# Batching and ending of a grouped convolution behind a chain of 18 pointwise layers

## The chip, the cores and the metric

The kernel runs on one core of one Trainium2 chip. The metric is the device time of one execution in microseconds (us). The engines are TensorE (PE, with its weight loads as PEld), VectorE (DVE), ScalarE (ACT), GpSimd (POOL) and SyncE (SP, which issues DMAs). All data is fp32.

## What is computed

The input `x` is 32 images of 14 x 14 pixels with 512 channels. Two layers follow each other, and each adds to its input:

```python
def layer0(x):                       # after a group norm of x, 32 groups
    anchors = []
    for i in range(18):
        nx = gelu(x @ block_w[i] + block_b[i])          # 512 x 512
        if i in (11, 14, 17):
            h = gelu(mean(nx) @ fc1_w[t] + fc1_b[t])
            gates = softmax((h @ fc2_w[t] + fc2_b[t]).reshape(-1, 3, 512), axis=1)
            nx = nx + gammas[t] * sum_a(gates[a] * anchors[a])
        x = nx
        if i in (1, 4, 9): anchors.append(x)
    return x
x = x + layer0(_gn(x))
x = x + conv3x3(_gn(x), W, groups=32)                   # SAME padding
```

`_gn` normalizes every image over each group of 16 channels.

## The kernel before, in words

**Blocks.** Channels lie on the 128 partitions, in four chunks `c` of 128; pixels lie on the free axis. A "tile" n is two images (392 pixels), a pair p is two tiles, so there are 8 pairs of 4 images. A block is one of the 18 layers for one pair; there are 144, and `steps` (lines 90 to 99) fixes their order: neighbouring pairs are interleaved so that the gating of one pair runs under blocks of the other. The last six blocks are 15 to 17 of pair 6 and then 15 to 17 of pair 7. A block multiplies 2 x 2 half matrices with 7 products in place of 8 (`block`, line 352): each product is 4 matmuls of 128 x 128 by 392 columns, and each fp32 matmul shows as two rows in the trace. ACT saves intermediate sums and applies the gelu, DVE adds PSUM into them (L403) and forms four differences of the inputs of the next block (L350). A `quarter` is a buffer of two chunks by 392 pixels; 35 of them serve everything that lives for a while.

**The calendar.** All other work is put by hand between the products. A block has seven ticks, one after each product, so the n-th block begins at tick 7n; `tend` is the tick after the last. `at(tick, fn)` books a function, and `put(first, {"dve": us, "act": us}, fn)` books it at the first tick from `first` on where the room of each engine named (`ROOM` per tick of a block, `TAIL` from `tend` on) still holds its estimate. At build time the ticks are run in order, so the calendar sets the order of the instructions on each engine's queue and on SP's, and each engine works its queue in order.

**Gating** (`plan_gates`, line 563). After a target layer (11, 14, 17), `gate_hidden` and `gate_logits` compute the gates from the pooled output; `gate_part` adds two of the three gated anchors on DVE, one image and one chunk at a time (L542), and `gate_last` scales the third on ACT (L554), added by `gate_add` (L561).

**End of a pair** (`plan_end`, line 651). After layer 17 the pair's input, kept in HBM (`xkeep`), is loaded and added (`load_residual`, `residual`, L605 and L609). DVE takes the statistics (`bn_stats` and `bn_aggr`, L183 and L184). Means and variances are averaged over groups by a matmul with a mask (`scales_mean`, `scales_rstd`), the power -0.5 is taken on POOL (L205), and a Newton step follows (`scales_newton`). ACT writes two sets of columns, `x` itself (L619) and the normalized one (L624), into an order that has the image column outermost, and two DMAs for each chunk and set (L636) write them to HBM, to `x2d` and `xnd`, once for the left and once for the right eight columns of the image. For the last pair these DMAs are issued by ACT, else by SP.

**Convolution.** A group of 16 input and 16 output channels with 8 image columns fills 128 rows; the filter row and the image column become a band matrix of 128 x 128 for each of the three filter rows. These bands are built once (`build_band`) and kept in HBM (`band`). A batch is half of the images (`NBAT` 2, 16 images), and a unit is one group of a batch, so there are 64 units. A unit loads its normalized columns, its `x` and its bands (L738, L745; for batch 1 the bands are loaded ahead by `load_bands`, L726), does six matmuls (L756, three filter rows for the left and right halves), adds `x` (L766), transposes (L780), and copies into an output tile on ACT (L787). After eight units, a chunk, ACT issues the output's DMAs (L794).

**Order of the units** (`plan_batch`, line 817, and lines 885 to 892). Batch 0, ready when pair 3 is done, has 32 units; 14 are spread over the blocks, and `NLATE` 18 run from `tend` on. Batch 1 is ready when pair 7 is done:

```python
        else:
            for j in range(NG // 2):
                at(a + 1 + j // 2, load_bands, j)
            for g in range(NG):
                plan_unit(m, g, b + 3 + g, 4)
```

Here `b` is one tick after the last columns of the last pair, so all 32 units follow it. Loads are booked three to eight ticks ahead, but not before their ring of buffers comes free: in `plan_unit` four for bands, five for normalized columns, six for `x`.

Of the kernel before, what the change touches and what calls it, by code (L numbers as in the profile page):

```python
# [19 lines left out]
def kernel(  # L20
# [84 lines left out]
    ROOM = {"dve": (1.5, 0.0, 3.3, 3.3, 1.2, 0.0, 0.0), "act": (1.0, 0.4, 1.5, 1.5, 0.8, 0.4, 0.0)}  # L105
    TAIL = {"dve": 4.0, "act": 3.6}
# [67 lines left out]

    def stats_tiles(name):
        st = small.tile([P, NR, 6], F32, tag="st", name=f"st_{name}")
        mv = small.tile([P, NR, 2], F32, tag="mv", name=f"mv_{name}")
        return {"st": st, "mv": mv}

    def stats_of(d, xc, c, n, images=range(NI)):  # L180
        for b in images:
            r = c * NB4 + n * NI + b
            nc.vector.bn_stats(d["st"][:, r, :], xc[:, b * HW : (b + 1) * HW])  # L183
            nc.vector.bn_aggr(d["mv"][:, r, :], d["st"][:, r, :])  # L184

    def scales_mean(d, name):
        mv = d["mv"]
        mps = aux(f"mps_{name}")
        nc.tensor.matmul(mps[:, :NR], lhsT=gmask, rhs=mv[:, :, 0], start=True, stop=True)
        mr = small.tile([P, 3, NR], F32, tag="mr", name=f"mr_{name}")  # L190
        nc.vector.tensor_copy(mr[:, 0], mps[:, :NR])
        v3 = small.tile([P, NR], F32, tag="v3", name=f"v3_{name}")
        nc.vector.tensor_sub(v3, mv[:, :, 0], mr[:, 0])
        nc.vector.tensor_mul(v3, v3, v3)
        nc.vector.tensor_add(v3, v3, mv[:, :, 1])
        d["mr"], d["v3"] = mr, v3

    def scales_rstd(d, name):

        vps = aux(f"vps_{name}")  # L200
        nc.tensor.matmul(vps[:, :NR], lhsT=gmask, rhs=d["v3"], start=True, stop=True)
        ve = small.tile([P, NR], F32, tag="ve", name=f"ve_{name}")
        nc.vector.tensor_scalar(ve, vps[:, :NR], 1e-5, None, ALU.add)
        y = small.tile([P, NR], F32, tag="y", name=f"y_{name}")
        nc.gpsimd.tensor_tensor(y, ve, mhalf, ALU.pow)  # L205
        d["ve"], d["y"] = ve, y

    def scales_newton(d, name):
        ve, y = d["ve"], d["y"]
        e = small.tile([P, NR], F32, tag="e", name=f"e_{name}")  # L210
        nc.vector.tensor_mul(e, y, y)
        nc.vector.tensor_mul(e, e, ve)
        nc.vector.tensor_scalar(e, e, -0.5, 1.5, ALU.mult, ALU.add)
        mr = d["mr"]
        nc.vector.tensor_mul(mr[:, 1], y, e)
        if name[0] == "b":
            nc.vector.scalar_tensor_tensor(
                mr[:, 2], mr[:, 0], -1.0, mr[:, 1], ALU.mult, ALU.mult
            )
# [56 lines left out]
    def plan_start(p):  # L276
# [16 lines left out]
        b = put(b + 1, {"dve": 0.8}, lambda: scales_mean(pst[p], f"a{p}"))  # L293
        b = put(b + 1, {"dve": 0.2}, lambda: scales_rstd(pst[p], f"a{p}"))
        b = put(b + 2, {"dve": 0.8}, lambda: scales_newton(pst[p], f"a{p}"))
# [147 lines left out]

    fcw = {}
# [46 lines left out]
    def gate_logits(k, t, name, box):  # L491
# [3 lines left out]
        for m in range(NCK, NL):  # L495
# [30 lines left out]
        gt = small.tile([P, NA, NC4], F32, tag="g", name=f"g_{name}")  # L526
        nc.vector.scalar_tensor_tensor(
            gt, ex, gam[:, t : t + 1], sm.unsqueeze(1).to_broadcast([P, NA, NC4]),
            ALU.mult, ALU.mult,
# [3 lines left out]
    def gate_part(p, box, h, n, d):  # L533

        gt = box["g"]
        c = h * NH + d
        for b in range(NI):
            sl = slice(b * HW, (b + 1) * HW)
            j = c * NB4 + n * NI + b
            o = box["nx"][h][n][:, d, sl]  # L540
            for a in range(NA - 1):
                nc.vector.scalar_tensor_tensor(  # L542
                    o, anc[p][a][h][n][:, d, sl], gt[:, a, j : j + 1], o, ALU.mult, ALU.add
                )

    def gate_last(p, i, box, h, n):

        gt = box["g"]
        q = box[h, n] = quarter(f"gq{h}{n}_{p}_{i}")
        for d in range(NH):  # L550
            for b in range(NI):
                sl = slice(b * HW, (b + 1) * HW)
                j = (h * NH + d) * NB4 + n * NI + b
                nc.scalar.activation(  # L554
                    q[:, d, sl], anc[p][NA - 1][h][n][:, d, sl], AF.Identity,
                    scale=gt[:, NA - 1, j : j + 1],
                )

    def gate_add(box, h, n):
        nx = box["nx"]  # L560
        nc.vector.tensor_tensor(nx[h][n], nx[h][n], box.pop((h, n)), ALU.add)  # L561

    def plan_gates(p, i):

        k = at_step[p, i]
        t1 = NP7 * (k + 1)
        name = f"{p}_{i}"
        ti = TARGETS.index(i)
        box = boxes[p, i] = {}
        end = k == len(steps) - 1  # L570
        if p == 0:
            at(t1 + 1, gate_differences, k, ti)
        at(t1 + (0 if end else 1), gate_hidden, k, ti, name, box)
        a = put(t1 + (1 if end else 2), {"dve": 2.6}, gate_logits, k, ti, name, box) + 1
        last = a
        for n in range(2):
            for h in range(2):
                b = put(a, {"act": 1.4}, gate_last, p, i, box, h, n)
                for d in range(NH):
                    last = max(last, put(a, {"dve": 1.65}, gate_part, p, box, h, n, d))  # L580
                last = max(last, put(b + 1, {"dve": 0.95}, gate_add, box, h, n))
        assert i == NB - 1 or last < NP7 * at_step[p, i + 1], (p, i, last)
        return last
# [3 lines left out]
    NBAT = 2  # L587
# [6 lines left out]
    x2d, xnd = [  # L594
        [
            [tc.dram_tile([2, P * KC, NV], F32, name=f"{v}{m}_{c}") for c in range(NCK)]
            for m in range(NBAT)
        ]
        for v in ("x2d", "xnd")
    ]  # L600

    def load_residual(p, n, h, d):
        t = 2 * p + n
        d[n, h] = quarter(f"xb_{t}_{h}")
        nc.sync.dma_start(d[n, h].rearrange("p c n -> p (c n)"), xkeep[t][h])  # L605

    def residual(n, h, p, d):
        nx = boxes[p, NB - 1]["nx"]
        nc.vector.tensor_add(nx[h][n], nx[h][n], d.pop((n, h)))  # L609

    def columns(p, c, n, d, mr=None):
# [3 lines left out]
        if n == 0:  # L615
            d[c] = qpool.tile([P, W, PV], F32, tag="q", name=f"xc{mr is None:d}_{p}_{c}")
        src = nx[c // NH][n][:, c % NH, :].rearrange("p (q w) -> p w q", w=W)
        if mr is None:
            nc.scalar.copy(d[c][:, :, n * NI * H : (n + 1) * NI * H], src)  # L619
        else:  # L620
            for b in range(NI):
# [3 lines left out]
                    d[c][:, :, q0 : q0 + H], src[:, :, b * H : (b + 1) * H], AF.Identity,  # L625
                    scale=mr[:, 1, r : r + 1], bias=mr[:, 2, r : r + 1],
                )
        if n == 0:
            return
        xc = d.pop(c)  # L630
        m, j = divmod(p, BP)
        dest = (x2d if mr is None else xnd)[m][c]
        for v in range(2):
            w0 = v * (W - KC)
            eng = nc.scalar if p == NPAIR - 1 else nc.sync
            eng.dma_start(  # L636
                dest[v].rearrange("(q k) v -> q k v", k=KC)[:, :, j * PV : (j + 1) * PV],
# [3 lines left out]
    def plan_residual(p, a):  # L641

        xb = {}
        last = a
        for h in range(2):
            for n in range(2):
                at(a - 2, load_residual, p, n, h, xb)
                last = max(last, put(a, {"dve": 1.0}, residual, n, h, p, xb))
        return last

    def plan_end(p, a):
        d, xc, xd = {}, {}, {}

        def stats(n, c):
            if not d:
                d.update(stats_tiles(f"b{p}"))
            stats_of(d, boxes[p, NB - 1]["nx"][c // NH][n][:, c % NH], c, n)

        at(a, anc.pop, p)
        if p < NPAIR - 1:  # L660
            a = plan_residual(p, a)
        last = a
        for c in range(NCK):
            for n in range(2):
                last = max(last, put(a, {"dve": 1.0}, stats, n, c))
        b = put(last + 1, {"dve": 0.8}, lambda: scales_mean(d, f"b{p}"))
        b = put(b + 1, {"dve": 0.2}, lambda: scales_rstd(d, f"b{p}"))
        b = put(b + 2, {"dve": 0.8}, lambda: scales_newton(d, f"b{p}"))
        b += 1
        for c in range(NCK):  # L670
            for n in range(2):
                put(a, {"act": 0.95}, columns, p, c, n, xc)
        for c in range(NCK):
            for n in range(2):
                b = put(b, {"act": 0.95}, lambda c=c, n=n: columns(p, c, n, xd, d["mr"]))
        return b
# [6 lines left out]
    band = [tc.dram_tile([P, 3 * P], F32, name=f"band{g}") for g in range(C // CG)]  # L683
# [12 lines left out]
    def build_band(g):  # L696
# [4 lines left out]
        tiles = [  # L701
            cvpool.tile(shape, F32, tag="xn", name=f"bt{v}_{g}", bufs=NXN) for v in range(2)
        ]
# [225 lines left out]
```

## Time and profile before

| what | value |
|---|---|
| median of 3 runs | 3023.99 us (3022.62 to 3025.87) |
| the profiled execution | 3026.72 us, span 3025.0 us |
| PE, PEld busy | 2940.5 us (97%), 1802.0 us (60%) |
| DVE, ACT, POOL busy | 1810.6 us (60%), 1520.8 us (50%), 47.9 us (2%) |
| mean granted TensorE clock | 0.990 |
| moved by DMA | 456.74 MB, mean 151 GB/s |

The span runs from the first to the last instruction of the core. The page shows it in 40 equal slices of about 76 us; a digit is the busy share of a slice in tenths, and `PEclk` is the clock that TensorE was granted. A row of busy times by stage gives, for a stretch of the span, the busy microseconds of each engine with the number of its instructions, then the clock (1.00 is full), the mean busy share of the 16 DMA engines, and GB/s. A row of the timeline gives start, duration, engine and line, operation, output and inputs, how many instructions it merges, and in brackets the idle time before it and what ended it. A row of groups gives busy time and mean duration in ns, and after the second bar the idle time before the group.

### The profile page before, as it was taken

How to read it: one execution, taken by the hardware profiler on the slowest of the kernel's cores; microseconds unless marked ns; L12 is line 12 of the kernel's file. 1: busy time of each engine (PE TensorE's matmuls, PEld its weight loads, DVE VectorE, ACT ScalarE, POOL GpSimd, SP SyncE). 2: the span in 40 equal slices, each digit the busy share in tenths (PEclk: the TensorE clock that was granted, in tenths of full speed). 3: DMA queues.
4: the chain of work that ended last, by engine and by line, in shares of the span. 5: the costliest groups of instructions: out<-in, count | busy, mean ns of one | idle time of the engine just before them, and what ended most of it. 6: DMA issues, size and time to landing. Idle time of an engine off the chain costs nothing.

```text
span 3025.0 us, 32202 instructions
## 1 busy us (share of the span) xinstructions
PE 2940.5 (97%) x9985; PEld 1802.0 (60%) x9985; DVE 1810.6 (60%) x3679; ACT 1520.8 (50%) x3603; POOL 47.9 (2%) x25
## 2 busy tenths in 40 slices
PE   7999999999999999999999999999999999999758
PEld 4555555555565555555565566666566655665657
DVE  5466565776567766776667564774557633666711
ACT  3444445556455555556455554555555554555442
POOL 0000000000000000000000000000000000000000
PEclk9999999999999999999999999999999999999979
DMA  4343334545454544645454444544446444334895
GB/s 141 120 146 132 126 118 156 182 126 151 151 160 140 164 128 142 190 129 155 134 165 144 146 129 138 190 125 142 134 140 191 139 141 131 124 127 137 256 284 165
DMA packets 404595, 456.74 MB, mean 151 GB/s; under 512 B 151899, under 2 KB 239050, under 8 KB 404426
## 3 DMA queue, kind: packets, MB, share of 16 engines
q1 hardware_dynamic: 361994, 437.38, 46.3%
q10 hardware_dynamic: 42432, 17.32, 2.3%
q8 instruction: 80, 1.31, 0.2%
q14 instruction: 89, 0.73, 0.1%
HBM read 372.83 MB, written 81.79 MB: 150 GB/s over the span
## 4 chain that ended last, share of the span: by engine, by line


## 5 line engine op out<-in xcount | busy, mean ns | idle before, releaser
L366 PE MATMUL x<-t,s 128*128 128x392 f32 x2304 | 808.1, 493 | 0.0
L379 ACT ACTIVATE o<-c,bias 128x392 f32<-128x392 f32 x720 | 440.2, 620 | 568.2 <-DVE c L403 551.7
L366 PEld LDWEIGHTS x<-t,s 128*128 128x128 f32 x2304 | 434.0, 190 | 306.1
L399 ACT COPY c<-x 128x392 f32<-128x392 f32 x576 | 279.5, 485 | 393.7 <-PE x L366 386.2
L366 PE MATMUL z<-t,s 128*128 128x392 f32 x1152 | 404.7, 494 | 0.0
L366 PE MATMUL x<-t,w 128*128 128x392 f32 x1152 | 402.7, 492 | 0.0
L366 PE MATMUL z<-o,s 128*128 128x392 f32 x1088 | 381.7, 494 | 0.0
L366 PE MATMUL y<-o,w 128*128 128x392 f32 x1088 | 381.4, 493 | 0.0
L366 PE MATMUL x<-o,w 128*128 128x392 f32 x1088 | 380.3, 492 | 0.0
L403 DVE TENSOR_TENSOR c<-x,c 128x392 f32<-128x392 f32 x288 | 160.0, 564 | 347.7 <-PE x L366 290.9
L403 DVE TENSOR_TENSOR c<-y,c 128x392 f32<-128x392 f32 x288 | 163.3, 567 | 330.5 <-PE y L366 223.2
L366 PEld LDWEIGHTS x<-t,w 128*128 128x128 f32 x1152 | 218.9, 190 | 160.3
L542 DVE SCALAR_TENSOR_TENSOR o<-o,g,o 128x196 f32<-128x196 f32 x768 | 298.7, 420 | 14.2
L366 PEld LDWEIGHTS z<-t,s 128*128 128x128 f32 x1152 | 216.0, 190 | 148.9
L350 DVE TENSOR_TENSOR t<-o,o 128x784 f32<-128x784 f32 x272 | 264.1, 971 | 67.4 <-ACT o L379 64.8
L366 PEld LDWEIGHTS x<-o,w 128*128 128x128 f32 x1088 | 206.6, 190 | 149.7
L366 PEld LDWEIGHTS z<-o,s 128*128 128x128 f32 x1088 | 204.7, 190 | 144.2
L366 PEld LDWEIGHTS y<-o,w 128*128 128x128 f32 x1088 | 204.6, 190 | 143.9
L350 DVE TENSOR_TENSOR t<-o,t 128x784 f32<-128x784 f32 x272 | 264.4, 972 | 5.5
L403 DVE TENSOR_TENSOR c<-z,c 128x392 f32<-128x392 f32 x288 | 158.8, 562 | 106.5 <-PE z L366 105.7
L399 ACT COPY c<-z 128x392 f32<-128x392 f32 x288 | 138.9, 482 | 162.8 <-PE z L366 162.4
L379 ACT ACTIVATE o<-x,bias 128x392 f32<-128x392 f32 x240 | 140.3, 585 | 91.6 <-PE x L366 85.0
(102 smaller groups left out, 1966.1 us busy)
## 6 DMA issues: line engine op xcount, KB each, us to landing
w<-in_L_conv_block_w_dram SPq DMA_DIRECT2D x144, 1024.0 KB
s<-skeep SPq DMA_DIRECT2D x504, 256.0 KB
skeep<-s SPq DMA_DIRECT2D x72, 256.0 KB
xn<-xnd SPq DMA_DIRECT2D x64, 224.0 KB
xs<-x2d SPq DMA_DIRECT2D x64, 224.0 KB
xkeep<-xt SPq DMA_DIRECT2D x32, 392.0 KB
xb<-xkeep SPq DMA_DIRECT2D x32, 392.0 KB
x2d<-xc SPq DMA_DIRECT2D x56, 224.0 KB
```

The source lines that it names most:

```text
L350: nc.vector.tensor_tensor(t[j], i0, i1, ALU.subtract)
L366: nc.tensor.matmul(acc[d][:, :N], lhsT=lhsT[:, kk, d * P : (d + 1) * P], rhs=rhs[:, kk, :], start=first and kk == 0, stop=kk == NH - 1, sk ...
L379: nc.scalar.activation(o[:, d, :], srcs[d], AF.Gelu_apprx_tanh, bias=bias[:, r : r + 1])
L399: nc.scalar.copy(cs[d], acc[d][:, :N])
L403: nc.vector.tensor_tensor(cs[d], acc[d][:, :N], cs[d], ALU.add)
L542: nc.vector.scalar_tensor_tensor(o, anc[p][a][h][n][:, d, sl], gt[:, a, j : j + 1], o, ALU.mult, ALU.add)
```

## The change

Six things change together.

1. **Four batches of 8 images, two groups a unit.** `x2d` and `xnd` become one array in which `x` and the normalized columns (index e) and the left and right half (v) lie side by side for each row, so that a unit needs one load. Each batch has 16 units of two groups; bands are kept for two groups together. Two band buffers and five buffers for columns serve all batches but the last, whose bands are loaded ahead.
2. **The last pair ends chunk by chunk**: gates, statistics, scales and columns of chunk 0, then of chunk 1, and so on; units of the last batch wait for their chunk only. All writes of columns are issued by SP.
3. **Gates on differences.** Since the gates sum to one, `gates @ anchors` is anchor 0 plus two gated differences. Anchors 1 and 2 are turned into differences in place, once for each pair; `gate_base` adds gamma times anchor 0 before the gates are known.
4. **x is added by a DMA** that accumulates into the output of the last layer, issued by POOL after `gate_base`.
5. **Statistics without `bn_aggr`**: the two halves that `bn_stats` gives go into the group sums, with two matmuls each.
6. **Room and late units**: `ROOM` and `TAIL` change, and 14 units of batch 2 run from `tend` on.

The diff, cut to its core:

```diff
-    ROOM = {"dve": (1.5, 0.0, 3.3, 3.3, 1.2, 0.0, 0.0), "act": (1.0, 0.4, 1.5, 1.5, 0.8, 0.4, 0.0)}
-    TAIL = {"dve": 4.0, "act": 3.6}
+    ROOM = {"dve": (1.7, 0.0, 3.4, 3.4, 1.7, 0.0, 0.0), "act": (1.0, 0.8, 1.5, 1.5, 1.0, 0.8, 0.8)}
+    TAIL = {"dve": 3.0, "act": 3.6}
...
-            nc.vector.bn_aggr(d["mv"][:, r, :], d["st"][:, r, :])
...
+    def group_sums(name, src, n):
+        ps = aux(name)
+        for v in range(2):
+            nc.tensor.matmul(
+                ps[:, :n], lhsT=gmask, rhs=src[:, :, v], start=v == 0, stop=v == 1
+            )
+        return ps[:, :n]
...
+    def anchor_difference(p, a, h, n):
+        v = anc[p][a][h][n]
+        nc.vector.tensor_tensor(v, v, anc[p][0][h][n], ALU.subtract)
+
+    def gate_base(p, i, h, n):
+
+        t = TARGETS.index(i)
+        o = boxes[p, i]["nx"][h][n]
+        nc.vector.scalar_tensor_tensor(
+            o, anc[p][0][h][n], gam[:, t : t + 1], o, ALU.mult, ALU.add
+        )
+
+    def gate_part(p, box, c, n, b):
+
+        h, d = divmod(c, NH)
+        sl = slice(b * HW, (b + 1) * HW)
+        j = c * NB4 + n * NI + b
+        o = box["nx"][h][n][:, d, sl]
+        nc.vector.scalar_tensor_tensor(
+            o, anc[p][1][h][n][:, d, sl], box["g"][:, 0, j : j + 1], o, ALU.mult, ALU.add
+        )
...
+        box["base"] = {
+            (h, n): put(t1, {"dve": 1.0}, gate_base, p, i, h, n) for h in range(2) for n in range(2)
+        }
+        return put(t1 + (1 if end else 2), {"dve": 2.2}, gate_logits, k, ti, name, box) + 1
+
+    def plan_gates(p, t, a, chunks):
+
+        box = boxes[p, t]
+        last = max(a, *box["base"].values())
+        for cs in chunks:
+            for n in range(2):
+                b = a
+                for c in cs:
+                    b = put(b, {"act": 0.75}, gate_last, p, t, box, cs, c, n)
+                for c in cs:
+                    for i in range(NI):
+                        last = max(last, put(a, {"dve": 0.43}, gate_part, p, box, c, n, i))
+                last = max(last, put(b + 1, {"dve": 0.5 * len(cs)}, gate_add, box, cs, n))
         return last
...
-    NBAT = 2
+    NBAT = 4
...
+    def residual(n, h, p):
+
+        nc.gpsimd.dma_start(
+            boxes[p, NB - 1]["nx"][h][n].rearrange("p c n -> p (c n)"),
+            xkeep[2 * p + n][h], accum_op=ALU.add,
+        )
...
+    def plan_end(p):
+
+
+        d = {}
+        for (h, n), tick in boxes[p, NB - 1]["base"].items():
+            at(tick, residual, n, h, p)
         if p < NPAIR - 1:
-            a = plan_residual(p, a)
-        last = a
+            a = gated[p] + 1
+            at(a, anc.pop, p)
+            return [plan_norm(p, d, a, list(range(NCK)))] * NCK
+        a = gated[p]
+        out = []
         for c in range(NCK):
...
+            b = plan_gates(p, NB - 1, a, [[c]])
+            if c == NCK - 1:
+                at(b + 1, anc.pop, p)
+            out.append(plan_norm(p, d, b, [c]))
+        return out
...
-    NXS, NXN, NBW = 6, 5, 4
...
+    NX, NBW = 5, 2
...
+    def unit_load(m, u):
+
+        c, ul = divmod(u, UC)
+        xs = cvpool.tile([P, 2, 2, 2 * NV], F32, tag="x", name=f"x_{m}_{u}", bufs=NX)
+        nc.sync.dma_start(
+            xs.rearrange("r g e n -> r g (e n)"),
+            x2d[m][c].rearrange("(g r) e v n -> r g (e v n)", r=P)[:, 2 * ul : 2 * ul + 2],
+        )
+        if m == NBAT - 1:
+            bw = bands.pop(u)
+        else:
+            bw = cvpool.tile([P, 2, 3, P], F32, tag="bw", name=f"bw_{m}_{u}", bufs=NBW)
             nc.sync.dma_start(
...
+                bw.rearrange("p g y d -> p (g y d)"), band[u].rearrange("p g n -> p (g n)")
+            )
+        units[m, u] = {"xs": xs, "bw": bw}
...
+        ready = ended[(m + 1) * BP - 1]
+        if m < NBAT - 1:
+            t0 = ready[-1] + 6
+            t1 = ended[(m + 2) * BP - 1][-1] if m < NBAT - 2 else tend - 4
+            early = NU - (NLATE if m == NBAT - 2 else 0)
+            for u in range(early):
+                plan_unit(m, u, t0 + (t1 - t0) * u // early, 8)
+            for j in range(NU - early):
+                left["dve"][tend + 1 + j] += 0.65
+                left["act"][tend + 2 + j] += 0.9
+                plan_unit(m, early + j, tend + j, 3)
         else:
-            for j in range(NG // 2):
-                at(a + 1 + j // 2, load_bands, j)
-            for g in range(NG):
-                plan_unit(m, g, b + 3 + g, 4)
+            tk = 0
+            for u in range(NU):
+                tk = max(tk + 1, ready[u // UC] + 3, tend + NLATE)
+                at(tend + (u - 6 if u < 6 else 3 + u // 2), load_bands, u)
+                plan_unit(m, u, tk, 3)
...
-    NLATE = 18
+    NLATE = 14
```

Here `plan_norm` books the statistics, scales and columns of the chunks that it is given, NU is 16 units of a batch, UC is 4 units of a chunk, and `ended` holds for each pair the tick of the last columns of each chunk.

## The prediction

> **What bounds the kernel now.** I read the page's slices first, then the busy time by stage, then the timeline of the end, then the groups by shape.
>
> ```profile
> PE   7999999999999999999999999999999999999758
> PEclk9999999999999999999999999999999999999979
> DMA  4343334545454544645454444544446444334895
> ```
>
> PE is full until about slice 37; only then do the DMA engines fill up and does PE fall back. So there are two stages with different bounds. By stage:
>
> ```profile
> core 0: us, PE busy (x) PEld busy (x) DVE busy (x) ACT busy (x) POOL busy (x), PEclk, DMA share, GB/s
> 75.00:2812.00 2737.00, 2736.55 (x8993) 1628.93 (x8993) 1700.58 (x3396) 1423.06 (x3287) 37.70 (x13) 1.00 0.46 145
> 2812.00:2835.00 23.00, 19.50 (x118) 17.99 (x119) 19.38 (x47) 9.62 (x38) 0.00 (x0) 1.00 0.70 205
> 2835.00:2920.00 85.00, 40.89 (x198) 35.78 (x196) 30.87 (x108) 38.69 (x96) 5.80 (x2) 0.75 1.00 258
> 2920.00:2985.00 65.00, 60.04 (x329) 57.99 (x330) 12.43 (x20) 16.14 (x80) 0.00 (x0) 0.90 0.95 285
> 2985.00:3025.00 40.00, 29.82 (x185) 28.89 (x183) 7.45 (x12) 9.30 (x52) 0.00 (x0) 0.91 0.31 83
> ```
>
> From 75 to 2812 us (the blocks) PE idles 0.45 us in 2737: DVE (62% busy) and ACT (52%) never end a wait that matters, so relief of them there is worth nothing, and **every PE instruction moved into this stage costs its full time**. The end is 213 us, from the last product at 2812 to 3025: until 2920 the DMA engines are full and PE is half idle, then PE runs 32 units in a row.
>
> ```profile
> 2861.99 2.65 SPq L745 DMA_DIRECT2D bw<-band  x1
> ...
> 2870.73 4.36 PE L756 MATMUL cps<-xn,bw 128*128 128x224 f32 x12 [3.57 <-DMA bw<-band]
> ...
> 2920.21 7.39 PE L756 MATMUL cps<-xn,bq 128*128 128x224 f32 x24 [21.34 <-DMA xn<-xnd]
> 2923.63 1.25 ACTq L636 DMA_DIRECT2D xnd<-xc  x2
> 2927.87 2.33 PE L756 MATMUL cps<-xn,bq 128*128 128x224 f32 x12
> ...
> 3011.43 2.33 PE L756 MATMUL cps<-xn,bq 128*128 128x224 f32 x12
> ...
> 3016.29 1.08 ACTq L794 DMA_DIRECT2D out_dram<-o  x1
> ```
>
> A load of bands issued at 2862 lets PE go on at 2870.7; PE then waits 21 us for normalized columns, because all of batch 1 (32 units) sits behind the last pair's columns (last write issued 2924). Units then come every 2.60 us (3008.83 to 3011.43, say), and from the last unit's matmuls to the end it is 13.6 us (2.6 of matmuls, 11.0 after).
>
> **The change, part by part.**
>
> *Units.* Before, 14 units of 64 run inside the blocks and 50 after. A unit after the change (two groups of 8 images) has the same 6 matmuls and 4 transposes as one before (one group of 16), so 64 again. Following the planner's arithmetic, batches 0 and 1 fit inside the blocks (32 units); batch 2 is ready early too, but only 2 of its 16 are placed there, 14 are kept for the end (NLATE). So 34 inside, 30 after: 20 units move into the full PE stage, **20 x 2.60 = +52 us**.
>
> *Group sums.* Mean and variance become two matmuls each: 2 more per set, some 15 sets inside the blocks. Such a matmul is two PE rows, 0.36 us at most (L189 in the timeline), 0.22 from start to start. 30 x 0.22 to 0.36 = 7 to 11 us; I take 7. The last product then ends at 2812 + 52 + 7 = 2871.
>
> *Vector and Scalar work.*
>
> ```profile
> L542 DVE SCALAR_TENSOR_TENSOR o<-o,g,o 128x196 f32<-128x196 f32 x768 | 298.7, 420 | 14.2
> L624 ACT ACTIVATE xc<-o,mr_b 128x196 f32<-128x196 f32 x128 | 85.1, 725 | 9.1 <-issue 9.1
> L619 ACT COPY xc<-o 128x392 f32<-128x392 f32 x64 | 55.0, 876 | 8.6 <-issue 8.6
> L184 DVE BATCH_NORM_AGGREGATE mv_a<-st_a 128x2 f32<-128x6 f32 x128 | 23.3, 182 | 4.4
> ```
>
> DVE loses 384 gate parts (161 us), 256 aggregates (47) and 32 additions of x (31); it gains 64 differences of anchors at 0.97 (62) and 96 base steps, which no row shows at this size: 0.97 (the 128x784 addition) to 4 x 0.42, so 93 to 161. Net 16 to 84 us less, all beside PE: 0. The planner allows DVE 10.2 us a block instead of 9.3; with its own 7.3 us (4 x 0.97 + 6 x 0.565) that is 17.5 of the block's 18.5, so the cover is thin, and I put 0 to 10 us of stalls into the range.
>
> *The accumulating DMA.* It replaces a plain load and an addition. The new wait: the first gate part stands at the head of DVE's queue until it has landed, with the additions of PSUM (L403), and so PE's banks, behind. Between base step and first gate part lie 4 ticks of 2.64 us = 10.5 us. No DMA from POOL is in the trace. Its packets are those of the load of x (3136 B, median 124 ns, 8 on each engine: 1.0 us, perhaps double for an accumulate). Here a rule speaks against the change: the Trainium skill (SBUF — State Buffer, "SBUF: two separate sides") says that one-source fp32 copies of VectorE in two-port mode lock GpSimd out of writing descriptors; the section after it tells of a POOL DMA of 620 ns that became 3100. At 4 us undisturbed (my estimate: the row, twice over, plus issue and landing as the 3.4 us of a band below) a fivefold 20 us would miss the slack by 10, for 7 pairs: 70 us. But the rows around it are DVE instructions with two inputs or a PSUM source (L350, L403, L542), which that page doesn't count as two-port ("Who interferes with whom"). I take 0, with 70 as the far bound; it is nearer 0. On POOL's queue the powers of the scales (2.90 us, L205) come behind it, due 14 ticks later and more: 0.
>
> *The end.* Per DMA, from the packet records of the trace (medians: 224 B 16 ns, about 18 in the mixed stretches; 512 B 27; 896 B 42; 1536 B 65; 2048 B 84; 3136 B 124) on 16 engines. The new unit load has 256 packets of 1792 B (75 ns between those rows): 1.20 us; two groups' bands 128 x 3072 B (121 ns): 0.97; a write of columns 1024 x 224 B: 1.15; an output 1568 x 512 B: 2.65. In the order of SP's queue, from the last product to the load of unit 7 of batch 3, which stands behind the last pair's last columns: 12 units of batch 2 (26.0), 8 loads of batch 3 (9.6), 10 bands (9.7), 32 writes of pairs 6 and 7 (36.8), 4 outputs (10.6), 4 accumulations (4.0): **96.7 us**. The same count over 2835 to 2920, dips included, gives 0.90 of the time, and 1.0 in pure reads (2930 to 2950); I take 0.94: 103 us. Plus 1.5 to start and 2 to land: 106.5. The last pair's writes leave ACT's queue (8 of x, 8 of the normalized; an issue held ACT 0.5 to 2.4 us) for SP's, which then waits for the columns with later unit loads behind; those are issued three ticks ahead, so 0 while the DMA queues are full.
>
> Nine units (7 to 15) are then left: 23.4 us, since their loads (1.2 each, an output per four) come faster than PE's 2.60. The first two run slow, as at 2920: 24 rows in 7.39 us instead of 4.6, +2.8. The skill (TensorE: Matmul & The Clock Gate, Part 1) releases the clock after about 3.4 us of work, which would make it some 1.7; the trace decides, 2.8. Before, PE lost another 8 us to output buffers in 32 units (2920.2 to 3013.8 less 83.2 and 2.8): +2 here. Last step 11.0. The end is 106.5 + 23.4 + 2.8 + 2 + 11.0 = **146 us** instead of 213.
>
> *Sum.* 2871 + 146 = 3017 against the span of 3025.0: 8 us less. The profiled execution took 3026.7, the median of the runs is 3024.0; 3024 - 8 = **3016 us**. Most of what the end gives back (67 us) the blocks pay (59).
>
> **Rivals.**
>
> *The DMA engines are not the bound of the end; ACT is.* For it: the new packets are long, and ACT was 45% busy from 2835 to 2920 with the columns in its in-order queue. ACT to the last columns: 15 copies x 0.876 + 32 x 0.725 + 16 gate parts x 0.375 + 17 units x 0.72 + 4 outputs of up to 2.6 + 0.5 = 66 us; with 12 of waits 78. Against it: SP's queue holds 97 us in the same stretch. 78 + 39 (the close) + 1.5 = 118; 2871 + 118 = 2989, so **2988 us**.
>
> *Slower: the two buffers for bands.* Before there were four. The load for unit u+2 may be issued only when unit u's matmuls are done, and SP's queue waits with it, writes and bands behind. A pair of units takes the landing time L plus its matmuls. The trace has L = 3.4 us (issued 2853.2, used 2856.6) and 8.7 (2862.0 to 2870.7, the clock low). It decides from 14 x (L + 3.4)/2 > 82 us (what the list above needs for these ticks), L above 8.3. Each load is twice as long and its neighbours too: with L = 11, 101 us, then 23 for the other chunks and 40 for the close: 164, 2871 + 164 = 3035, so **3034 us**.
>
> *It does less than it says:* were the 14 late units of batch 2 also run inside, the blocks would pay 36 more for about as much less; so "four batches" is in fact 20 units.
>
> **How the numbers follow.** Full DMA queues 0.50 (3016; with a pace of 0.85 to 1.0, 3008 to 3028), ACT 0.23 (2988), two band buffers 0.24 (3034), stalls in the blocks by the accumulating DMA 0.03 (over 3045). A measurement here tells 0.2% (6 us) from no change. Faster: 0.30 of the first and 0.23 = 0.53; same 0.16; slower 0.04 + 0.24 + 0.03 = 0.31. The range goes from a little under the ACT case to the band case with 9 us of stalls: 2985 to 3043; the likeliest alone 3008 to 3028.
>
> **What would show it.** The last block product near 2871 with PE still idle for about nothing before it: right on the blocks; later means stalls of DVE. DMA share near 1.0 for 100 us after it, and nine units at 2.6 us to finish: right on the end. ACT without gaps and DMA share under 0.8 there: the first rival. PE waiting on bands for several us again and again: the second. DVE waiting on x in the gate parts: the accumulating DMA. I'd be wrong outright if units in the blocks don't cost PE their 2.60 us.

## The result and the profile after

| | before | after |
|---|---|---|
| median (runs) | 3024.93 us (3022.62 to 3027.95, 4) | 3042.70 us (3040.94 to 3045.52, 4) |
| ratio to before, 95% interval | | 1.0059 [1.0042, 1.0076] |
| profiled execution, span | 3026.72 us, 3025.0 us | 3045.52 us, 3043.8 us |
| the last row of the blocks' last product begins | 2810.4 us | 2891.5 us |
| from there to the end of the span | 214.6 us | 152.3 us |

The change made the kernel 17.8 us slower where I had forecast 8 us faster. The end became 62 us shorter (forecast 67), but the blocks became 81 us longer (forecast 59). So the first place to look is the blocks. The slices of the page after the change, PE, its clock and DMA:

```profile
PE   7999999999999999999999999999999999989967
...
PEclk9999999999999999999999999999999999999988
DMA  4343336544455436654456444655446543433597
```

PE is full for longer (to slice 38), with one 8 in slice 36 (2663 to 2739 us). That digit is the first sign: nothing in the plan empties PE there. By stage (start and end of the stretch, its length, busy time of each engine with instructions, clock, DMA share, GB/s):

```profile
core 0: us, PE busy (x) PEld busy (x) DVE busy (x) ACT busy (x) POOL busy (x), PEclk, DMA share, GB/s
75.00:2892.00 2817.00, 2800.52 (x9358) 1688.53 (x9357) 1655.08 (x2998) 1429.53 (x3294) 63.16 (x42) 1.00 0.48 150
2892.00:2920.00 28.00, 16.77 (x98) 15.75 (x97) 11.73 (x36) 13.67 (x30) 5.90 (x5) 0.82 1.05 250
2920.00:2990.00 70.00, 47.47 (x227) 44.21 (x226) 20.32 (x70) 28.44 (x60) 3.08 (x3) 0.80 1.06 288
2990.00:3044.00 54.00, 38.73 (x220) 36.44 (x218) 10.63 (x26) 14.21 (x40) 1.01 (x1) 0.89 0.63 182
```

In the blocks PE now idles 16.5 us (2817 less 2800.5) where it had idled 0.45, although DVE is less busy than before (1655 us in a longer stretch against 1701). Three instances of one pattern make all of it (gaps of 3.97, 6.26 and 6.26 us; in the first it is a unit's matmul that waits, for an addition of DVE). The waits of the last 250 us of the blocks (engine, its operation and line, what it waited for, total, times, longest) hold two rows that belong together:

```profile
DVE t L355 <- PE z L371: 20.8, 3, 6.9
...
PE x L371 <- ACT c L404: 12.5, 2, 6.3
```

The second of them in the timeline, in block 136 (layer 13 of pair 7; rows that are not on the path are left out):

```profile
2728.55 2.80 PE L371 MATMUL z<-t,s 128*128 128x392 f32 x8
2731.38 0.97 DVE L355 TENSOR_TENSOR t<-o,o 128x784 f32<-128x784 f32 x1 [6.92 <-PE z L371]
2732.46 0.97 DVE L355 TENSOR_TENSOR t<-o,t 128x784 f32<-128x784 f32 x1
2733.35 0.42 DVE L558 SCALAR_TENSOR_TENSOR o<-o,g,o 128x196 f32<-128x196 f32 x1
2733.80 0.97 DVE L581 TENSOR_TENSOR o<-o,gq 128x784 f32<-128x784 f32 x1
2734.70 1.03 DVE L408 TENSOR_TENSOR c<-y,c 128x392 f32<-128x392 f32 x2
2735.35 1.14 ACT L384 ACTIVATE o<-c,bias 128x392 f32<-128x392 f32 x2 [10.62 <-DVE c L408]
2736.39 0.79 ACT L572 ACTIVATE gq<-o,g 128x196 f32<-128x196 f32 x2
2737.09 0.84 ACT L404 COPY c<-x 128x392 f32<-128x392 f32 x2
2737.60 4.91 PE L371 MATMUL x<-t,s 128*128 128x392 f32 x8 [6.26 <-ACT c L404]
```

Read it from the top. DVE waits 6.92 us for product z of this block before it may write a pre-add `t<-o,o`, though its two inputs are outputs of the block before, ready long ago. What it waits for is not data but the buffer. Behind it on DVE's queue stands the addition of product y (L408). Behind that, on ACT, stands a gelu that needs it (10.62 us), and behind the gelu the save of product x (L404). PE may not go on until x is saved. After the gap, eight rows take 4.91 us instead of 2.80: the granted clock is at half there (0.50, the third number from the end):

```profile
2737.60:2741.60 4.00, 4.00 (x6) 2.19 (x7) 3.90 (x9) 3.20 (x9) 0.00 (x0) 0.50 0.00 0
```

In the kernel before, the third pre-add of block 136 ran ahead of product z and waited for nothing:

```profile
2656.06 0.97 DVE L350 TENSOR_TENSOR t<-o,o 128x784 f32<-128x784 f32 x1
...
2663.24 2.80 PE L366 MATMUL z<-t,s 128*128 128x392 f32 x8
```

Block 136 lasts 27.0 us instead of 18.4, 133 takes 27.7 instead of 20.6, and 139 takes 27.8 instead of 18.4. That is 25.1 us in all.

In the built program the addresses tell which buffer it is. `pre_adds` takes four of the 35 quarters for each block. In blocks 133, 136 and 139 of the changed kernel the third (t2) is given the memory of the **first (t0) of the same block**, whose last reader is product z. In the kernel before, the third got one that had come free in the block before. In both kernels all 35 quarters are taken at this point, but in the changed one two of them hold gate parts of ACT (`gq`) that wait for their addition; before, none did.

### The profile page after: what moved, and what is told of

Its sections match the earlier page's. It is cut to its first block, busy times and chain, and to the rows that moved or that the text cites. A ratio compares the mean times of both kernels' runs of the same rounds, so it can differ in the third digit from the quotient of the medians.

```text
span 3043.8 us, 31589 instructions
## 1 busy us (share of the span) xinstructions
PE 2959.1 (97%) x10073; PEld 1819.1 (60%) x10073; DVE 1735.0 (57%) x3209; ACT 1510.9 (50%) x3475; POOL 77.6 (3%) x60
## 4 chain that ended last, share of the span: by engine, by line
PE 96%; DMA 2%; DVE 1%; SPq 0%; ACT 0%; issue 0%; POOL 0%; DVEq 0%; ACTq 0%
PE x L371 50%; PE z L371 25%; PE y L371 12%; PE cps L797 5%; PE lps L503 1%; DMA bw<-band 1%; PE tpo L821 1%; PE tpi L249 1%; PE hps L487 1%; DMA x<-x2d 0%; DMA w<-in_L_conv_block_w_dram 0%; DMA out_dram<-o 0%; DVE t L355 0%; SPq L668 0%; SPq L776 0%; DVE st_a L187 0%
## 5 line engine op out<-in xcount | busy, mean ns | idle before, releaser
L404 ACT COPY c<-x 128x392 f32<-128x392 f32 x576 | 278.3, 484 | 367.8 <-PE x L371 360.8
L408 DVE TENSOR_TENSOR c<-x,c 128x392 f32<-128x392 f32 x288 | 160.7, 564 | 489.2 <-PE x L371 400.5
L408 DVE TENSOR_TENSOR c<-y,c 128x392 f32<-128x392 f32 x288 | 162.5, 566 | 294.0 <-PE y L371 199.4
L355 DVE TENSOR_TENSOR t<-o,o 128x784 f32<-128x784 f32 x272 | 264.1, 971 | 96.7 <-ACT o L384 61.9
L355 DVE TENSOR_TENSOR t<-o,t 128x784 f32<-128x784 f32 x272 | 264.3, 972 | 11.3 <-PE x L371 6.0
L404 ACT COPY c<-z 128x392 f32<-128x392 f32 x288 | 139.2, 484 | 195.4 <-PE z L371 194.8
L408 DVE TENSOR_TENSOR c<-z,c 128x392 f32<-128x392 f32 x288 | 161.1, 564 | 125.0 <-PE z L371 124.8
L391 ACT ACTIVATE o<-c,bias 128x196 f32<-128x196 f32 x288 | 129.5, 450 | 95.2 <-DVE c L408 95.2
```

Of the source, the lines that this page charges most:

```text
L355: nc.vector.tensor_tensor(t[j], i0, i1, ALU.subtract)
L391: nc.scalar.activation(o[:, d, sl], srcs[d][:, sl], AF.Gelu_apprx_tanh, bias=bias[:, r : r + 1], accum_out=pooled[:, c, m : m + 1],)
L404: nc.scalar.copy(cs[d], acc[d][:, :N])
L408: nc.vector.tensor_tensor(cs[d], acc[d][:, :N], cs[d], ALU.add)
```

## The experiments

**Theory.** The pool of quarters is full in the late blocks: the gates' ScalarE parts (`gq`) are now booked ahead of the additions that give their quarters back, so t2 must wait for t0. That costs about 22 us, and the rest of the forecast stands. **Rivals:** DVE has too little slack (my own worry in the prediction); the accumulating DMA; two band buffers in the end (my second rival).

In the table, "last product" is the start of the last row of the blocks' last product in the profiled execution, and "end" is from there to the end of its span. A single profile's end scatters by some microseconds.

| kernel | median us (runs) | ratio to before, 95% | last product | end |
|---|---|---|---|---|
| after | 3042.7 (4) | 1.0059 [1.0042, 1.0076] | 2891.5 | 152.3 |
| after, 36 quarters | 3018.2 (11) | 0.9977 [0.9968, 0.9986] | 2866.2 | 154.3 |
| after, 3 band buffers | 3039.4 (5) | 1.0048 [1.0035, 1.0061] | 2888.6 | 149.0 |
| after, plain load of x | 3050.5 (4) | 1.0081 [1.0068, 1.0095] | 2897.1 | 151.6 |
| 36 quarters, one output left out | 3011.1 (5) | 0.9954 [0.9942, 0.9967] | 2867.5 | 144.5 |
| after, gate parts behind additions | 3018.8 (21) | 0.9980 [0.9973, 0.9986] | 2865.8 | 148.4 |
| 36 quarters, shared bands | 3004.6 (5) | 0.9931 [0.9918, 0.9943] | 2866.1 | 136.9 |
| 36 quarters, 8 late units | 3026.4 (13) | 1.0005 [0.9997, 1.0013] | 2882.0 | 140.1 |
| 36 quarters, last pair at once | 3022.0 (13) | 0.9994 [0.9986, 1.0002] | 2865.5 | 154.2 |
| before, 34 quarters | 3024.9 (11) | 1.0001 [0.9992, 1.0010] | 2809.8 | 210.5 |
| gate parts behind, 3 band buffers | 3018.7 (11) | 0.9977 [0.9968, 0.9985] | 2865.1 | 153.2 |
| 36 quarters, shared bands, 16 late | 3002.6 (5) | 0.9926 [0.9913, 0.9938] | 2860.1 | 139.4 |
| gate parts behind, shared, 16 late, 6 x | 3001.7 (4) | 0.9919 [0.9906, 0.9933] | 2861.0 | 138.8 |

**One more quarter.**

```diff
-    qpool = ctx.enter_context(tc.tile_pool(name="qpool", bufs=35))
+    qpool = ctx.enter_context(tc.tile_pool(name="qpool", bufs=36))
```

> The changed kernel with 36 quarter buffers in place of 35, nothing else. Theory (the full pool): the third pre-add of blocks 133, 136 and 139 was written into the buffer that the first pre-add of the same block had just given back, so it waited for product z; with a 36th buffer it takes one that is free long before. The three DVE waits of 6.9 us behind z go, the two waits of PE for ACT of 6.3 us go, these blocks last 18.4 to 20.6 us instead of 27 to 28, the last product of the blocks comes about 22 us earlier (2869 instead of 2891), and the time is about 3021 us (3014 to 3028), within 0.3% of the kernel before. Rival (DVE has too little slack in the late blocks, by its added work or its order): the buffers change nothing, the waits stay or move by a block, 3039 to 3046 us. Second rival (all of the excess was made in the end, by band buffers): no change of the total beyond 5 us, since the end then ends as late.

Measured: 3018.2 us. The block of the stall above, the pre-adds and PE, now:

```profile
2713.28 2.80 PE L371 MATMUL x<-o,w 128*128 128x392 f32 x8
2713.49 0.97 DVE L355 TENSOR_TENSOR t<-o,t 128x784 f32<-128x784 f32 x1 [0.40 <-PE x L371]
2715.92 2.80 PE L371 MATMUL y<-o,w 128*128 128x392 f32 x8
2716.12 0.98 DVE L355 TENSOR_TENSOR t<-o,o 128x784 f32<-128x784 f32 x1 [1.66 <-PE x L371]
2717.20 0.97 DVE L355 TENSOR_TENSOR t<-o,t 128x784 f32<-128x784 f32 x1
...
2718.55 2.80 PE L371 MATMUL x<-t,s 128*128 128x392 f32 x8
2721.18 2.80 PE L371 MATMUL z<-t,s 128*128 128x392 f32 x8
```

The third pre-add (2716.12) runs under product y, ahead of product z. It waits for a product x of this block's start instead of for z, and PE waits for nothing. The three blocks last 20.6, 18.4 and 18.4 us, as before the change, and the last product comes 25.3 us earlier. The blocks give the whole gain of 24.5; the end is the same within its scatter.

**The gates' parts behind the additions, 35 quarters.** The same buffers as the changed kernel, another booking:

```diff
+        free = a
         for cs in chunks:
             for n in range(2):
-                b = a
+                b = free if len(cs) > 1 else a
...
-                last = max(last, put(b + 1, {"dve": 0.5 * len(cs)}, gate_add, box, cs, n))
+                free = put(b + 1, {"dve": 0.5 * len(cs)}, gate_add, box, cs, n)
+                last = max(last, free)
```

> The changed kernel with its 35 quarters, but the planner books a gate's ScalarE part of one pair of chunks no earlier than the addition of the one before it, so that fewer quarters hold such parts at one time; the same instructions in another order. In the build no third pre-add takes the buffer of the first of its block any more. Theory (the full pool, filled by the gates' ScalarE parts that are now booked ahead of their additions): as good as the 36th quarter, 3014 to 3023 us, no stall in blocks 133, 136 and 139. Rival (the 36th buffer helped in another place, such as the columns or the bands in the end): 3035 to 3043 us.

Measured: 3018.8 us; no wait of DVE's pre-adds for z is left. In the built program one gate part instead of two holds a quarter when the third pre-add of block 136 takes its own. Two independent edits, one of memory and one of order, take away the same 24 us. The DVE work is the same in both, so the slack of DVE was not what ran out.

**The kernel before with one quarter less** (`bufs=34`).

> The kernel before with 34 quarter buffers instead of 35. In the build no third pre-add takes the buffer of the first of its block, so the kernel before had a buffer to spare. Theory (what costs time is not a full pool as such but a third pre-add in the buffer of the first): the time of the kernel before, 3021 to 3030 us, no block of 27 us. Rival (any kernel with its pool full in the late blocks loses about 20 us): 3040 to 3050 us.

Measured: 3024.9 us, blocks 133, 136 and 139 of 20.6, 18.4 and 18.4 us. So the kernel before had a quarter to spare. Its pool is full at these blocks all the same, with 35 quarters and with 34, so neither a smaller pool nor a full one costs anything by itself. Only the pairing of t2 with t0 does.

**x by a plain load** for pairs 0 to 5 (pairs 6 and 7 keep the accumulating DMA):

```diff
-            at(tick, residual, n, h, p)
+            if p >= NPAIR - 2:
+                at(tick, residual, n, h, p)
...
+                        at(a - 2, load_residual, p, n, h, xb)
+                        last = max(last, put(a, {"dve": 1.0}, add_residual, n, h, p, xb))
```

> The changed kernel with x of the pairs 0 to 5 added as before: a plain load into quarters at the tick two ahead of the gates' end and four DVE additions per pair, instead of the accumulating DMA (pairs 6 and 7 keep the accumulating DMA, where quarters are short). Theory: the slack of four ticks covers the accumulating DMA wholly, so there was no wait to take away: 3040 to 3046 us, the last product within 2 us of 2891. Rival (the accumulating DMA holds up DVE or ACT in the late blocks of each pair): 5 to 20 us faster, spread evenly over the pairs.

Measured: 3050.5 us, 7.8 slower; my "0" was off, in the direction that clears the accumulating DMA. The blocks end 5.6 us later. The gap of block 133 is 2.3 us longer (6.26 instead of 3.97), and four small gaps of PE add 1.1. The granted clock is also at half for two stretches of 3.4 us, at 613 and 1688 us, without a gap before them; why is open. In the changed kernel itself no gate part waits for x. The groups of the base step, of the gate parts and of the accumulation (line, engine, operation, count, busy time and mean ns, then the idle time before them), and the row of the page for these DMAs (count, KB each, median us from issue to landing):

```profile
L558 DVE SCALAR_TENSOR_TENSOR o<-o,g,o 128x196 f32<-128x196 f32 x384 | 139.7, 415 | 0.0
L548 DVE SCALAR_TENSOR_TENSOR o<-o,gam,o 128x784 f32<-128x784 f32 x96 | 94.8, 1028 | 1.0 <-ACT o L391 0.9
```

```profile
o<-xkeep POOLq DMA_DIRECT2D x32, 392.0 KB, 6.9
```

384 gate parts idle 0.0 us before them. The DMA lands after 6.9 us, inside the slack of 10.5.

**Three band buffers**, with the stalls and without.

```diff
-    NX, NBW = 5, 2
+    NX, NBW = 5, 3
```

> The changed kernel with three band buffers instead of two, 35 quarters as it has. Rival of two band buffers: the 31.9 us in which PE waits for bands in the end fall to 10 or less and the time falls by 15 to 25 us, to 3018 to 3028. Theory (the DMA list sets the end to about 2990, whatever the buffers): the same bytes move at the same rate, the waits only change their name from bands to x, 3037 to 3043 us; the three stalls in the blocks stay.

> The changed kernel with the gate's ScalarE parts booked behind the addition before (35 quarters, 3018.8 us) and three band buffers instead of two. Theory (the list of bytes sets the end): 1 to 5 us faster, as with the three stalls in place: 3014 to 3018 us, and PE's waits change from bands to x. Rival of two band buffers: most of the 36 us of PE's waits for bands go and the time falls to 3006 or less.

Measured: 3.3 us with the stalls (2.9 of them ahead of the end, and the two intervals overlap), 0.1 without. In the end PE waits for bands, and this looks like my second rival. First the changed kernel, then the same with three buffers:

```profile
PE cps L797 <- DMA bw<-band: 31.9, 8, 8.9
...
PE cps L797 <- DMA x<-x2d: 7.5, 3, 4.2
```

```profile
PE cps L797 <- DMA bw<-band: 24.4, 6, 6.5
PE cps L797 <- DMA x<-x2d: 10.2, 5, 3.4
```

The waits shrink by 7.5 us on bands and grow by 2.7 on x, and the time hardly follows. A wait of 32 us on a buffer's load was not worth 32 us. The DMA share of 1.05 to 1.06 in this stretch suggests why: the queues behind it were full.

**Fewer bytes.** One kernel leaves out the output of images 16 to 23 (3.2 MB, so its result lacks them), and one lets the 14 late units of batch 2 use the band quarters that batch 3 loads anyway (5.5 MB less, nothing left out):

```diff
-        if ul == UC - 1:
+        if ul == UC - 1 and m != NBAT - 2:
```

```diff
         if m == NBAT - 1:
             bw = bands.pop(u)
+        elif u in bands:
+            bw = bands[u]
...
+                at(tend + j - 3, load_bands, early + j)
                 plan_unit(m, early + j, tend + j, 3)
...
-                at(tend + (u - 6 if u < 6 else 3 + u // 2), load_bands, u)
+                if u < NU - NLATE:
+                    at(tend + NLATE - 3 + u, load_bands, u)
```

> The changed kernel with 36 quarters, and the output of images 16 to 23 isn't written (four writes of 0.8 MB of ScalarE's queue left out, all of them at the end of the blocks or after; the units themselves are still worked). Theory (the end is set by the DMA list until the last pair's columns are written): 3.2 MB less at the 380 KB/us that the end moves make the end 6 to 9 us shorter than that of the kernel with 36 quarters alone. Rival (PE's units behind band buffers and the queue's order set the end): within 2 us of it.

> The changed kernel with 36 quarters, and the 14 late units of the third batch take the band quarters that the fourth batch loads anyway (loaded ahead of the late unit and kept), so that 14 loads of 393 KB go. Theory (the end is set by the list of DMA bytes): 5.5 MB less at the 380 KB/us of the full queues is 14 us, 3001 to 3010 us where 36 quarters alone gave 3018; the waits of PE for bands fall under 10 us. Rival (the end is set by the chain of the last pair, DVE and ScalarE): within 5 us of 3018.

Measured: 7.1 and 13.6 us faster than 36 quarters alone, 8.4 and 14.5 by the bytes. (The 380 KB/us is the trace's 121 ns for a packet of 3072 B on 16 engines, times the pace of 0.94 that I had used; with its shorter packets the end as a whole moves 250 to 290.) For an output's packets of 512 B the prediction's own list gives 11.3 us (4 x 2.65 / 0.94), so the first kernel gained less than that. The second also frees the late units from the two band buffers and alone could not tell bytes from buffers; the first leaves the buffers as they are, and a third buffer gained 0.1. So it is mostly bytes, not buffers, that set the end. What PE waits for in the kernel with shared bands:

```profile
PE cps L799 <- DMA x<-x2d: 25.8, 10, 8.6
```

The waits for bands are gone, a longer wait for x has come, and the time still fell by about what the bytes give: the name of the wait says only which load happened to be late.

**Units in or out** (`NLATE` 8 instead of 14).

> The changed kernel with 36 quarters and 8 late units of the third batch instead of 14, so that 6 more units are worked within the blocks. Theory: 6 x 2.60 us = 15.6 us more in the blocks (last product at 2882 instead of 2866), and 6 x 1.05 MB = 6.3 MB less in the end, at 380 KB/us 16.6 us: the time is 3017 us, within 6 us of that of 36 quarters alone. Rival (late units cost nothing in the end, since they fill the waits for the last pair's chain): 3028 to 3035 us. Rival (the blocks had room for units after all): 3002 to 3008 us.

Measured: 3026.4 us, 8.2 slower than 36 quarters, between the first two forecasts. In the profile the blocks pay 15.8 us (6 x 2.60 = 15.6, right) and the end gives back 14.2, 2.4 us a unit. The median says that it gives back less, some 7.4; the profiled execution (3023.8) was one of the quicker of the 13. Either way a unit inside the blocks costs more than it gives.

**The last pair at once.**

```diff
-        if p < NPAIR - 1:
+        if p < NPAIR - 1 or ONCE:
             a = gated[p] + 1
+            if p == NPAIR - 1:
+                a = plan_gates(p, NB - 1, gated[p], [[0, 1], [2, 3]]) + 1
```

> The changed kernel with 36 quarters and the last pair ended as one, like the pairs before it: gates of two chunks at a time, one set of scales over all four chunks, all columns after it; the work and the bytes are the same. Theory: the ending chunk by chunk puts the last pair's columns ahead by the time of the chain; without it the fourth batch's first loads come when nothing else is left for the DMA queues, and the time rises by 12 to 30 us, to 3030 to 3048. Rival (the list of bytes sets the end in either order): 3014 to 3024 us.

Measured: 3022.0 us. Ending chunk by chunk is worth 3.8 us, not the 12 to 30 that I expected. PE then waits 20.5 us in one piece for the last pair's first columns, but the batch's loads follow with nothing ahead of them, and its 16 units run at 2.6 us in a row, but for the first one or two.

**A version that beats both.**

> The changed kernel with 36 quarters, shared bands (3004.6 us) and all 16 units of the third batch after the blocks instead of 14. Theory: 2 x 2.60 us less in the blocks, 2 x 0.66 MB (x and output; the bands are shared) more in the end, at 380 KB/us 3.5 us: 3003 us, within 4 us of the kernel with shared bands. Rival (late units fill waits of the end and cost nothing there): 2999 us. Rival (each late unit costs its whole transfer with the bands, 2.8 us, and order): 3005 to 3008 us.

> A version put together from the parts: 35 quarters with the gate's ScalarE parts booked behind the addition before, shared bands, 16 late units, six x buffers and one band buffer (bands of late units are in quarters). Theory (the list of bytes sets the end, x buffers only move the waits): 2997 to 3004 us. Rival (five x buffers hold the loads back; PE waits 25.8 us for x in the end with shared bands): 2985 to 2994 us.

Measured: 3002.6 and 3001.7 us. The second has 35 quarters with the gate parts behind the additions, shared bands, 16 late units, six x buffers and one band buffer. It is 0.8% faster than the kernel before and some 1.3% below the median of the changed one. The six x buffers add nothing that can be told from the other version.

## Why the prediction was wrong, point by point

- **Blocks: units and group sums, right.** 20 units and 30 more sums were to cost 59 us. With the stalls gone the last product is 55.8 us later than before (2866.2 less 2810.4); 34 units instead of 14 are inside, and the sums grew by 6.7 us. The blocks also began 2.5 us sooner.
- **DVE and ACT: the step that failed.** I wrote that "the cover is thin, and I put 0 to 10 us of stalls into the range", having added DVE's microseconds against a block's length. The microseconds were covered; with the same work and 36 quarters nothing stalls. What ran out was buffers that come free in time. The prediction looked up no pool but the bands', although the change books the gates' ScalarE parts, each in a quarter, ahead of the additions that free them: two of the 35 hold such parts where the kernel before had none, and t2 is left with the buffer of t0. The stalls cost 24.5 us by the medians. Without this term the forecast of 3016 stands beside a measured 3018.2, in part by luck: the blocks came out 3 us shorter than forecast and the end 5 to 7 longer.
- **The accumulating DMA: right.** I had taken 0 and named 70 as the far bound by the Trainium skill (SBUF — State Buffer, "SBUF: two separate sides"), whose rule on VectorE's hold on GpSimd's descriptors would multiply it. It landed in 6.9 us, 1.7 times my undisturbed estimate of 4, not five times; undoing it for six pairs made the kernel slower. Whether an instruction that locks in that way ran meanwhile, no run here shows.
- **The end: right mechanism, mis-sized by 5 to 7 us.** I gave 146 us, counted from a point 1.6 us later than the table's; from there it took 150.7, and 152.6 with 36 quarters. The DMA share is 1.05 to 1.06 for 98 us (2892 to 2990), against 103 forecast, but the queues are not done then. By the packet records the 16 engines had 119 us of work each until the load of unit 7 landed (2892 to 3009.8), where my list had 96.7, or 103 with its pace: the unit loads took 29.4 us instead of 24.0, the writes of columns 41.5 instead of 36.8, five outputs 15.2 where I had four at 10.6, the accumulations 9.1 instead of 4.0, and the bands 22.8 instead of 21.3. In this stretch also lies the path of the last columns, which I had counted with "2 to land" (the second column is the duration):

```profile
2994.40 5.04 ACT L658 ACTIVATE xc<-o,mr_b 128x196 f32<-128x196 f32 x8
...
2999.47 1.31 SPq L668 DMA_DIRECT2D x2d<-xc  x2
...
3000.89 6.42 SPq L776 DMA_DIRECT2D x<-x2d  x4
...
3009.77 2.50 PE L797 MATMUL cps<-x,bq 128*128 128x224 f32 x6 [4.21 <-DMA x<-x2d]
...
3033.13 2.33 PE L797 MATMUL cps<-x,bq 128*128 128x224 f32 x12
...
3037.55 0.58 ACTq L831 DMA_DIRECT2D out_dram<-o  x1
```

```profile
2990.00:3000.00 10.00, 8.11 (x50) 7.54 (x49) 3.80 (x15) 7.08 (x16) 1.01 (x1) 1.00 0.54 149
2999.50:3009.80 10.30, 4.40 (x27) 3.82 (x26) 1.24 (x2) 1.60 (x6) 0.00 (x0) 0.91 1.06 289
```

  SP's queue waits 6.0 us for ACT's last columns (in two pieces, between 2985 and 3001), which I had put at 0, and the DMA share falls to 0.54. From the last write's issue to the unit that uses it are then 10.3 us, through HBM and back, with the share at 1.06 again. So unit 7 of the last batch starts 118 us after the blocks instead of 106.5. The nine units and the close then take 34 us (3009.8 to 3043.8) where I had 39: the first unit took 5.1 us and the others 2.6 each, none waited for an output buffer, and the last step was 8.1 instead of 11.0.
- **Rivals.** ACT as the bound: no; the DMA share is over 1 while ACT is 41% busy (28.4 of 70 us). Two band buffers: the sign that I named came (PE waits 31.9 us for bands), but a third buffer gave 0 to 3 us, so the sign did not mean what I took it to mean. "Less than it says": worked out from the 1.2 (by the median) to 2.4 us (by the profile) a unit above, the 20 units moved would make 25 to 48 of the 62 us of the end and the chunk-by-chunk ending 4; that sum was not run as such.
- **Direction.** I had given 31% to slower, but only 3% to stalls in the blocks, and those to another cause. The cause lay in the blocks, where I had looked at engines and queues only. That 3042.7 lies just inside my range (2985 to 3043) is luck: its upper end was the case of two band buffers with 9 us of stalls, and neither is what happened.

Open: the whole change in the end was tested by parts of it, not by putting the old batches into the new kernel, and the 7.8 us of the plain load of x are explained only in part.

## What to carry to other kernels

When a change moves a producer ahead of the work that frees its buffer, count the live buffers at the busiest point against the pool, not only the microseconds on each engine. A full pool alone cost nothing here; where it is full, look up which buffer the next tile gets and when the last reader of that buffer runs, because a late reader turns into a wait on an engine that looks idle. In the trace such a wait has a sign of its own: an instruction whose inputs are old waits for another that made none of them, here `t<-o,o` for z. And where the DMA queues are full, the name and length of an engine's wait for one load don't say what another buffer would bring; taking bytes away does.

## What the runs showed of the hardware that I had not expected

- A gap on PE cost more than its length. In block 136 a gap of 6.26 us cost 8.4: the eight rows after it took 4.91 us instead of 2.80, the eight after those 2.80 again, and the granted clock stayed at half for 4.1 us after the gap. In blocks 133 and 139 it stayed at half for 5.8 us after gaps of 3.97 and 6.26 us, and the blocks lost 7.1 and 9.4. So these stalls were 2 to 3 us dearer than their gaps.
- A packet of the accumulating DMA took 256 ns (median, 3136 B) where the plain load of x before the change took 124 for the same bytes.
- The power on POOL takes 1.02 us for 128 x 4 and 2.92 for 128 x 16, so four sets of scales cost it 4.1 us in place of 2.9, not four times as much:

```profile
L214 POOL TENSOR_TENSOR y_a<-ve_a,mhalf 128x16 f32<-128x16 f32 x8 | 23.4, 2923 | 608.3 <-DVE ve_a L213 608.3
...
L214 POOL TENSOR_TENSOR y_b<-ve_b,mhalf 128x4 f32<-128x4 f32 x4 | 4.1, 1023 | 86.8 <-DVE ve_b L213 86.8
```
